# Weight loads of the software DMA queue over 15 engines instead of 14

## The chip, the cores and the metric

The kernel runs on one core of one Trainium2 chip. The metric is the device time of one execution in microseconds (us). Before the change it is 749.29 us, the median of three runs (747.64 to 749.32). A profiled execution is a run of its own, and its time stands beside its span below.

## The reference

For each of 1024 samples there are 32 fields of 128 numbers. For each of the 496 pairs of fields (i, j) with i < j there is a 128 x 128 weight matrix. Field i is multiplied by the matrix of the pair, and the result is multiplied, number by number, with field j. Everything is float32.

```python
v_i = inputs[:, I_IDX, :]
v_j = inputs[:, J_IDX, :]
transformed = jnp.einsum('bpd,ped->bpe', v_i, W)
return transformed * v_j
```

The output has 1024 x 496 x 128 numbers, 260 MB; inputs and weights together are 49 MB.

## The kernel before, in words

**Tiles.** The host lays the fields out as `xt` (32 fields, each 128 x 1024: embedding on the partitions, samples along the row) and the weights as `wt`: 62 chunks of 8 pairs, each chunk 128 partitions x 8 x 128, that is 4 KB a partition and 512 KB in all. A pair q is worked on in two halves of 512 samples; the loop variable u counts the halves, 992 of them. The output of four pairs is gathered in one tile `ot` (128 x 4 x 1024, 16 KB a partition) and stored with one transfer of 2 MB.

**Work on a pair.** From the 16th pair on, each matrix and each field is split into two parts whose products are exact enough: ScalarE and GpSimd make the parts of a weight chunk in `split_w` (L141 to L145), two pairs at a time, and those of a field in `split_x` (L159 to L161). `first` (L223) has TensorE do two matmuls into PSUM and ScalarE scale the sum; `second` (L239), three halves later, adds the third matmul, and VectorE multiplies the finished 128 x 1024 with field j into the output tile (L255). Stores are issued on ScalarE's queue two halves later (L282). The order of all of this is written out by hand in one loop (L264 to L298); nothing is reordered afterwards.

**Output tiles.** There are three fixed tiles and, for a part of the time, four more, which lie in the room of field groups that are loaded late (`XAT`, L38: at pairs 52, 141, 219 and 313 one of them begins to be filled with fields). So from seven at the start the number of output tiles falls to three. `out_tile` takes the one whose last use is longest ago; VectorE's write into it waits until its last store has landed.

**Weight loads.** Three buffers hold weight chunks. The first chunks are loaded at times fixed in `w_at`; from chunk 12 on a chunk is loaded when GpSimd has finished splitting the one whose buffer it takes (`ring`, `spent`, L288 to L296). A whole chunk is one transfer on SyncE's queue (L125): 128 rows of 4 KB. The 25 chunks in `WAPART` (12, 14, ... 60) are loaded in two parts by `load_apart` (L106): the first `ROWS` = 8 x 14 = 112 partitions by GpSimd's software queue (L107), with the source seen as 14 x 8 rows, and the last 16 partitions by SyncE (L108). The host reorders the rows of these chunks to match.

**The cursor.** `move_on(k)` (L102, L104) issues a small transfer on the software queue: 2k rows of 64 bytes into the tile `mark`, seen as k x 2 rows. Nothing reads `mark`. It is issued once with k = 5 before the first such load, with k = 16 - 14 = 2 a few pairs after every load but the last (the list `back`, filled in the ring's code with the pair number plus `BACK`), and with k = 13 after the last. The sum of all k and of all 14s is 416 = 26 x 16.

Of the kernel before, what the change touches and what calls it, by code (L numbers as in the profile page):

```python
# [30 lines left out]
XLEAD = 5  # L31

XG = 4
NE = 14
ROWS = 8 * NE
WAPART = tuple(range(12, 62, 2))
BACK = 3
# [13 lines left out]
def kernel(  # L51
# [22 lines left out]
    nc = tc.nc  # L74
# [12 lines left out]
    def load_x(f, pieces=1, eng=None):  # L87
        if f == 0:

            t = rpool.tile([P, WL, P], F32, tag="w", name="x_0").rearrange("p q e -> p (q e)")  # L90
        else:
            t = xpool.tile([P, BT], F32, tag=f"x{f}", name=f"x_{f}")
        s = BT // pieces
        for k in range(pieces):
            (eng or nc.sync).dma_start(out=t[:, k * s : (k + 1) * s], in_=xt[f, :, k * s : (k + 1) * s])
        x_sb[f] = t

    w_raw = {}

    mark = xpool.tile([32, 16], F32, tag="mark", name="mark")  # L100

    def move_on(k):  # L102

        nc.gpsimd.dma_start(out=mark[: 2 * k], in_=xt[0, : 2 * k, :16].rearrange("(b a) n -> a b n", a=k))  # L104

    def load_apart(dst, src):  # L106
        nc.gpsimd.dma_start(out=dst[:ROWS], in_=src[:ROWS].rearrange("(b a) m n -> a b m n", a=NE))  # L107
        nc.sync.dma_start(out=dst[ROWS:], in_=src[ROWS:])  # L108
# [3 lines left out]
    def load_group(k, m):  # L112
        if m == XG - 1:
            group[k] = xpool.tile([P, XG, BT], F32, tag=f"g{k}", name=f"x_g{k}")
        f = XG * k + 1 + m
        x_sb[f] = group[k][:, m, :]
        nc.sync.dma_start(out=x_sb[f], in_=xt[f])

    def load_w(c, splits=(0, WL), eng=nc.sync):
        w_raw[c] = rpool.tile([P, WL, P], F32, tag="w", name=f"w_{c}")  # L120
        if c in WAPART:
            load_apart(w_raw[c], wt[c])
            return
        for a, b in zip(splits, splits[1:]):
            eng.dma_start(out=w_raw[c][:, a:b, :], in_=wt[c, :, a:b, :])  # L125
# [97 lines left out]
    def first(u):  # L223
        q, h = divmod(u, 2)
        i, c = pairs[q][0], q // WC
        r = slice(q % WC * P, (q % WC + 1) * P)
        s = slice(h * HB, (h + 1) * HB)
        if h == 0:
            po[q] = ppool.tile([P, BT], F32, tag="po", name=f"po_{q}")
        if q < nq0:  # L230
            nc.tensor.matmul(po[q][:, s], w_raw[q // WL][:, q % WL, :], x_sb[i][:, s], start=True, stop=True)  # L231
        else:
            for t in (0, 1):
                m = nc.tensor.matmul(po[q][:, s], w_s[c][t][:, r], x_s[i][t][:, s], start=t == 0, stop=t == 1)  # L234
                apart(m, scaled.get(u - 1) if h else None)
            scaled[u] = nc.scalar.mul(po[q][:, s], po[q][:, s], 1.0 + EPS)  # L236
            apart(scaled[u], taken.get(q - PB), "TensorE's products, which this waits for, have waited for it")

    def second(u):  # L239
        q, h = divmod(u, 2)  # L240
        i, j = pairs[q]
        r = slice(q % WC * P, (q % WC + 1) * P)
        s = slice(h * HB, (h + 1) * HB)
        if q >= nq0:
            m = nc.tensor.matmul(  # L245
                po[q][:, s], w_s[q // WC][2][:, r], x_s[i][2][:, s], start=False, stop=True, skip_group_check=True
            )
            apart(m, scaled[u ^ 1])
        g, k = divmod(q, OG)
        if k == 0 and h == 0:  # L250
            ots[g] = out_tile(g)
        if q >= NQ - 2:
            nc.vector.tensor_tensor(ots[g][:, k, s], po[q][:, s], x_sb[j][:, s], ALU.mult)  # L253
        elif h == 1:
            taken[q] = nc.vector.tensor_tensor(ots[g][:, k, :], po.pop(q), x_sb[j], ALU.mult)  # L255
        if q >= NQ - 2:
            stores.append((u + SLAG, out[g, :, k, s], ots[g][:, k, s]))
        elif g == 0 or q >= NQ - OG:
            if h == 1:
                stores.append((u + SLAG, out[g, :, k], ots[g][:, k]))  # L260
        elif k == OG - 1 and h == 1:
            stores.append((u + SLAG, out[g], ots[g]))

    for u in range(2 * NQ + LAG + SLAG):  # L264
        q = u // 2
        if u < 2 * NQ:
            i, j = pairs[q]
            if u % 2 == 0 and j == i + 1 and XG * ngroup < i - 2 - XLEAD:
                load_x(i - 2 - XLEAD)
            first(u)  # L270
            if u == 2 * nq0:
                move_on(5)
            if u % 2 == 0 and q in group_at:
                load_group(*group_at[q])
            if u % 2 == 1 and q in w_at:
                load_w(w_at[q])
            if u % 2 == 0 and q in back:
                move_on(16 - NE if max(w_raw) < WAPART[-1] else 13)
        if LAG <= u < 2 * NQ + LAG:
            second(u - LAG)  # L280
        while stores and stores[0][0] <= u - LAG:
            nc.scalar.dma_start(*stores.pop(0)[1:])  # L282
        if u % 2 == 1:
            ready = [t for t in todo if t[0] <= q]
            if ready:
                ready[0][2](u)
                todo.remove(ready[0])
        if ring[WB:] and ring[0] in spent:  # L288
            ring.pop(0)
            c = ring[WB - 1]  # L290
            if c == "x":
                load_x(0)
            else:
                load_w(c)
            if c in WAPART:
                back.append(q + BACK)  # L296
        while later and later[0][0] <= u:
            nc.vector.tensor_tensor(*later.pop(0)[1:], ALU.subtract)  # L298
# [31 lines left out]
```

## Time and profile before

| | |
|---|---|
| median of three runs | 749.29 us |
| the profiled execution, its own time | 743.81 us |
| span of the profiled execution, first to last instruction | 742.0 us |
| mean granted TensorE clock | 0.991 |
| moved by DMA | 310.04 MB, 418 GB/s over the span |
| stores of 2 MB on ScalarE's queue | 122, 13.2 us from issue to landing (median) |
| weight loads on the software queue | 25 of 448 KB, 11.8 us to landing; issue 0.622 us of GpSimd |
| their rest on SyncE's queue | 25 of 64 KB, 6.1 us to landing |
| cursor moves on the software queue | 26, 9.8 us to landing; issue 0.637 us of GpSimd on average |

How to read the profile: it starts with the busy time of each engine, then shows the span in 40 slices. In the row DMA each digit is the mean busy share of the core's 16 DMA engines in tenths. Part 3 lists the DMA queues: q10 is ScalarE's, which carries the stores, q1 SyncE's, which carries most loads, q0 the software queue of GpSimd, q8 and q14 fetch instructions. A line of the waits reads: who waited, for whom, the time in total, how often, and the longest single wait in us. A line of the windows reads: the stretch, its length, each engine's busy time with its count of instructions (PE, PEld, DVE, ACT, POOL), the granted clock, the DMA share and GB/s. PE is TensorE, DVE VectorE, ACT ScalarE, POOL GpSimd, SP SyncE. The trace also has a record for every DMA packet (start, duration, queue, size; not the DMA engine that moved it) and the time of each of the 16 landings of every transfer.

### The profile page before, as it was taken

Reading aid. Unit: us, or ns where it says so; the run is one execution under the profiler, and the core shown is the slowest. Engines: PE = TensorE matmul, PEld = TensorE weight load, DVE = VectorE, ACT = ScalarE, POOL = GpSimd, SP = SyncE. Lnnn points to the kernel's source line nnn. Section 1 sums busy time; section 2 is a strip of 40 time slices with the busy share of each in tenths; the row PEclk is TensorE's granted clock in tenths of the full one; section 3 lists DMA queues with packets and bytes.
Section 4 is the critical chain, followed back from the end, with each engine's and each line's share of the span. In section 5 each row is a group of like instructions: output and inputs, shape, how many; then the busy total and the mean of one; then the engine's idle time right before and its main releaser. Section 6 shows DMA issues by size and latency. Waiting matters only on the chain.

```text
span 742.0 us, 10650 instructions
## 1 busy us (share of the span) xinstructions
PE 703.8 (95%) x2946; PEld 549.4 (74%) x2946; DVE 636.8 (86%) x550; ACT 634.9 (86%) x1256; POOL 594.8 (80%) x882
## 2 busy tenths in 40 slices
PE   7999999999999999999899979999999999999994
PEld 3577777777878887776687758867878778777783
DVE  4888999999999998987798868977999899888885
ACT  1298999999999999898899968988989999998893
POOL 1789999999999999887778866977797878797660
PEclk9999999999999999999999999999999999999998
DMA  9999999999999999999999998999999999999998
GB/s 347 427 424 428 427 427 425 430 423 426 427 419 426 423 424 425 425 423 422 425 428 422 428 423 334 420 423 423 423 425 422 426 423 415 430 421 422 424 408 351
DMA packets 34667, 310.04 MB, mean 418 GB/s; under 512 B 5296, under 2 KB 5424, under 8 KB 18992
## 3 DMA queue, kind: packets, MB, share of 16 engines
q10 hardware_dynamic: 19584, 261.10, 83.4%
q1 hardware_dynamic: 10592, 36.77, 12.3%
q0 software_dynamic: 4432, 11.48, 3.9%
q8 instruction: 24, 0.39, 0.2%
q14 instruction: 35, 0.29, 0.1%
HBM read 49.29 MB, written 260.05 MB: 417 GB/s over the span
## 4 chain that ended last, share of the span: by engine, by line
PE 61%; DMA 23%; DVE 8%; POOL 3%; issue 2%; ACT 1%; DVEq 0%; ACTq 0%; POOLq 0%
PE po L234 38%; DMA out_dram<-ot 23%; PE po L245 19%; DVE ot L255 6%; PE po L231 4%; DVE xd L298 2%; POOL wd L145 1%; POOL wl L143 1%; POOL xl L160 1%; ACT po L236 0%; DMA x<-in_xt_dram 0%; POOL xl L161 0%; POOL wd L144 0%; DVE ot L253 0%; ACT wh L141 0%
## 5 line engine op out<-in xcount | busy, mean ns | idle before, releaser
L236 ACT ACTIVATE po<-po 128x512 f32<-128x512 f32 x962 | 553.4, 584 | 76.3 <-PE po L234 60.3
L255 DVE TENSOR_TENSOR ot<-po,x 128x1024 f32<-128x1024 f32 x358 | 429.8, 1220 | 70.9 <-DMA out_dram<-ot 23.8
L234 PE MATMUL po<-xh,wh 128*128 128x512 f32 x962 | 382.4, 398 | 20.1 <-DVE ot L255 19.1
L245 PE MATMUL po<-xd,wd 128*128 128x512 f32 x962 | 376.3, 391 | 4.8 <-DVE ot L253 2.4
L234 PE MATMUL po<-xl,wl 128*128 128x512 f32 x962 | 377.1, 392 | 1.4 <-POOL wl L143 1.0
L234 PEld LDWEIGHTS po<-xh,wh 128*128 128x128 f32 x962 | 181.2, 188 | 78.3 <-DVE ot L255 41.7
L143 POOL TENSOR_TENSOR wl<-w,wh 128x256 fp32r<-128x256 f32 x241 | 185.2, 768 | 66.1 <-ACT wh L141 60.0
L245 PEld LDWEIGHTS po<-xd,wd 128*128 128x128 f32 x962 | 181.1, 188 | 45.2 <-DVE ot L253 3.2
L234 PEld LDWEIGHTS po<-xl,wl 128*128 128x128 f32 x962 | 181.3, 188 | 41.0 <-POOL wl L143 4.0
L145 POOL TENSOR_TENSOR wd<-wl,wd 128x256 fp32r<-128x256 f32 x241 | 181.4, 753 | 20.1
L255 DVE TENSOR_TENSOR ot<-po,x_g 128x1024 f32<-128x1024 f32 x136 | 164.0, 1222 | 25.9 <-DMA out_dram<-ot 9.7
L144 POOL TENSOR_SCALAR wd<-wh 128x256 fp32r<-128x256 f32 x241 | 101.9, 423 | 20.5
L141 ACT ACTIVATE wh<-w 128x256 fp32r<-128x256 f32 x241 | 98.7, 410 | 5.7 <-DVE ot L255 3.6
L298 DVE TENSOR_TENSOR xd<-xh,xl 128x512 fp32r<-128x512 f32 x52 | 48.5, 934 | 0.0
L160 POOL TENSOR_TENSOR xl<-x_g,xh 128x512 fp32r<-128x512 f32 x32 | 41.5, 1297 | 3.2 <-ACT xh L159 2.9
L160 POOL TENSOR_TENSOR xl<-x,xh 128x512 fp32r<-128x512 f32 x20 | 25.8, 1290 | 15.7 <-ACT xh L159 15.4
L161 POOL TENSOR_SCALAR xl<-xl 128x512 fp32r<-128x512 f32 x52 | 34.4, 662 | 4.6
L231 PE MATMUL po<-x,w 128*128 128x512 f32 x60 | 28.4, 630 | 3.9 <-DMA x<-in_xt_dram 3.9
L231 PEld LDWEIGHTS po<-x,w 128*128 128x128 f32 x60 | 11.6, 199 | 19.9 <-issue 13.7
L159 ACT ACTIVATE xh<-x 128x512 fp32r<-128x512 f32 x20 | 12.3, 624 | 11.4 <-DMA x<-in_xt_dram 11.3
L159 ACT ACTIVATE xh<-x_g 128x512 fp32r<-128x512 f32 x32 | 20.0, 624 | 0.0
L104 POOL DMA_DIRECT2D mark<-in_xt_dram x26 | 16.6, 637 | 0.0
(7 smaller groups left out, 19.9 us busy)
## 6 DMA issues: line engine op xcount, KB each, us to landing
out_dram<-ot ACTq DMA_DIRECT2D x122, 2048.0 KB, 13.2
w<-in_wt_dram SPq DMA_DIRECT2D x36, 512.0 KB, 11.1
w<-in_wt_dram POOLq DMA_DIRECT2D x25, 448.0 KB, 11.8
x_g<-in_xt_dram SPq DMA_DIRECT2D x16, 512.0 KB, 17.0
x<-in_xt_dram SPq DMA_DIRECT2D x14, 512.0 KB, 9.5
out_dram<-ot ACTq DMA_DIRECT2D x6, 512.0 KB, 8.3
w<-in_wt_dram SPq DMA_DIRECT2D x26, 64.0 KB, 6.1
x<-in_xt_dram ACTq DMA_DIRECT2D x4, 256.0 KB, 5.7
```

The costliest lines, as they stand in the source:

```text
L141: halved[c] = nc.scalar.mul(h, raw, 1.0 - 2.0**-13)
L143: nc.gpsimd.tensor_tensor(l, raw, h.bitcast(F32), ALU.subtract)
L144: nc.gpsimd.tensor_scalar(d, h.bitcast(F32), EPS, 1.0, ALU.mult, ALU.mult)
L145: nc.gpsimd.tensor_tensor(d, l.bitcast(F32), d.bitcast(F32), ALU.subtract)
L160: nc.gpsimd.tensor_tensor(l, x_sb[f][:, s], h.bitcast(F32), ALU.subtract)
L161: nc.gpsimd.tensor_scalar(l, l.bitcast(F32), 1.0 / EPS, 1.0, ALU.mult, ALU.mult)
L231: nc.tensor.matmul(po[q][:, s], w_raw[q // WL][:, q % WL, :], x_sb[i][:, s], start=True, stop=True)
L234: m = nc.tensor.matmul(po[q][:, s], w_s[c][t][:, r], x_s[i][t][:, s], start=t == 0, stop=t == 1)
L236: scaled[u] = nc.scalar.mul(po[q][:, s], po[q][:, s], 1.0 + EPS)
L245: m = nc.tensor.matmul(po[q][:, s], w_s[q // WC][2][:, r], x_s[i][2][:, s], start=False, stop=True, skip_group_check=True)
L255: taken[q] = nc.vector.tensor_tensor(ots[g][:, k, :], po.pop(q), x_sb[j], ALU.mult)
L298: nc.vector.tensor_tensor(*later.pop(0)[1:], ALU.subtract)
```

## The change

The number of engines `NE` goes from 14 to 15. With it `ROWS` becomes 120, so GpSimd's queue loads 120 partitions of a split chunk, seen as 15 x 8 rows, and SyncE's queue the last 8. The move after each load becomes `move_on(1)`, for which a branch of its own issues a transfer of one number (4 bytes); the last move becomes 12 instead of 13. The first stays at 5. The host's reordering follows `NE`.

```diff
-NE = 14
+NE = 15
 ROWS = 8 * NE
...
     def move_on(k):
 
-        nc.gpsimd.dma_start(out=mark[: 2 * k], in_=xt[0, : 2 * k, :16].rearrange("(b a) n -> a b n", a=k))
+        if k == 1:
+            nc.gpsimd.dma_start(out=mark[:1, :1], in_=xt[0, :1, :1])
+        else:
+            nc.gpsimd.dma_start(out=mark[: 2 * k], in_=xt[0, : 2 * k, :16].rearrange("(b a) n -> a b n", a=k))
...
             if u % 2 == 0 and q in back:
-                move_on(16 - NE if max(w_raw) < WAPART[-1] else 13)
+                move_on(16 - NE if max(w_raw) < WAPART[-1] else 12)
```

## The prediction

> **What bounds the kernel now.** I read the page's slices first, then the DMA part, the waits, the critical chain, and last the packet records and landings of the trace.
>
> ```profile
> span 742.0 us, 10650 instructions
> PE 703.8 (95%) x2946; PEld 549.4 (74%) x2946; DVE 636.8 (86%) x550; ACT 634.9 (86%) x1256; POOL 594.8 (80%) x882
> ...
> DMA  9999999999999999999999998999999999999998
> ...
> q10 hardware_dynamic: 19584, 261.10, 83.4%
> q1 hardware_dynamic: 10592, 36.77, 12.3%
> q0 software_dynamic: 4432, 11.48, 3.9%
> ```
>
> The DMA row is 9 in all slices but two, and the three data queues fill 99.6% of the 16 engines. PE is at 95%, but the waits say that it is held, through DVE, by stores that have not yet landed:
>
> ```profile
> PEld po L234 <- DVE ot L255: 41.7, 58, 5.8
> DVE ot L255 <- DMA out_dram<-ot: 33.5, 32, 6.3
> PE po L234 <- DVE ot L255: 19.1, 24, 5.4
> ```
>
> A store lands only when its last engine is done, so the slowest engine matters, not the mean. The DMA view of 125 to 440 us gives the rate and the depth of the queue:
>
> ```profile
> DMA packets 13999, 133.73 MB, mean 425 GB/s; under 512 B 2340, under 2 KB 2340, under 8 KB 6992
> ...
> out_dram<-ot ACTq DMA_DIRECT2D x55, 2048.0 KB, 17.3
> ```
>
> A store of 2 MB is issued every 315 / 55 = 5.7 us and lands 17.3 us after its issue: three are in flight at a time, and no engine runs dry.
>
> The records name no engine, but a packet's start follows the end of the one before it on its engine by -4, -3 or 2 ns, and each engine must do 8 rows of every store. That lets me put the packets of 64 to 440 us into sixteen chains, none with an idle gap over 20 ns. What they show:
>
> - fourteen chains: a 16 KB store row takes 611 ns in the median, 613.6 in the mean; a 4 KB row 159 ns.
> - the two chains that get no rows of the split weight loads (I call them S and T; they also carry the two packets of the cursor move). S is slow before any load is split (64 to 125 us: mean 626 ns, against 612 on the others) and after (648). T is as fast as the others before (615, median 611); after, the mean is 649 with the median still 611: it is held now and then.
> - what S and T lost to long packets from 125 to 440 us is 16.9 and 16.7 us; of the others none lost over 2.9. The relief in that time is 14 loads x 7 rows x 0.155 us = 15.2 us. So T's relief goes into being held, and S's pays for its slowness: S stays 2 to 4 rows behind the median chain from 150 us on.
>
> At 435 us a straggler (one of the fourteen, 6 to 7 rows behind) holds a store, DVE waits 6.3 us, and PE comes back at a lower clock:
>
> ```profile
> 435.00:440.00 5.00, 2.56 (x12) 1.78 (x10) 0.42 (x1) 3.14 (x7) 4.50 (x9) 1.00 0.98 414
> 440.00:445.00 5.00, 2.02 (x5) 1.65 (x6) 3.28 (x4) 0.58 (x1) 0.43 (x1) 0.65 1.02 437
> 445.00:450.00 5.00, 5.00 (x17) 3.95 (x16) 2.90 (x3) 2.85 (x6) 0.79 (x2) 0.66 0.50 213
> ```
>
> The columns after the engines are clock, DMA share and GB/s. So late landings cost time here; the fourteen loaded engines and S set the pace together.
>
> **What the Trainium skill says.** All from the page DMA: Bandwidth & Descriptors.
> - Section "Why a DMA increments its semaphore by 16 and not by 1": the slowest dimensions of the two access patterns give the number k of engines; the software queue takes k consecutive ones from a round-robin cursor, SP's and ACT's queues the lowest-numbered k. The trace agrees for the software queue: fourteen chains with 8 rows per load, the same two without, and five chains with a marker at 36 us, both S and T among them. If the cursor starts at 0, the first move of 5 marks engines 0 to 4, the loads skip 3 and 4, and {S, T} = {3, 4}; no run shows the start.
> - Section "Queues, rings and completion order": an engine takes its queues in turn, by packets. The trace agrees: in a chain the rows of q0 and q1 stand between those of q10. A row more on one engine is then time more on it.
> - Section "Latency and other measured facts": engines 7 and 15 are usually the slower ones, with a guessed cause. The trace has one such chain, S, and no number for it.
> - Section "Where 436 GB/s comes from": a ceiling of 435 GB/s; 425 here, 98% of it.
>
> **The change, part by part.**
> 1. Instructions. The order on every engine is the same; shapes alone differ. POOL's issues of the load and of the move keep their places: 25 x 0.622 us and 26 x 0.637 us. The 4-byte move may cost less than the 4 rows or as much; nothing says more, 24 x (-0.1 to +0.1) us = -2.4 to +2.4 us on POOL, which is busy 80%. I take 0; what covers it is POOL's lead on its weight splits: PE waited for them for 4.0 + 1.0 us in all. Uncovered it would cost those 2.4 us at most. SP issues 8 rows instead of 16 (0.326 us each, on an otherwise idle queue): nothing. The move waits for the marker before it, 22 us old with a landing of 9.8: no wait, and the weight splits queued behind it on POOL are not held.
> 2. Rows. Per load of 128 rows, before: fourteen engines 8 + 1, two engines 1. After: fifteen engines 8, one none, and SP's 8 rows on engines 0 to 7, one each. So engines 0 to 7 keep 9 (the spared one 1), engines 8 to 15 go from 9 to 8, and the engine that loses its relief goes from 1 to 9: + 25 x 8 x 0.155 = 31 us of packets. The upper eight lose 25 x 0.155 = 3.9 us each. The sum of bytes is the same.
> 3. Who loses the relief. After the first move of 5, a load of 15 skips only the fifth of the marked engines, and 15 + 1 = 16 brings the cursor back to the same place, so it is always that one; the fourth now gets rows. The fourth is S or T.
> 4. If it is S. A loaded chain's nominal work: 122 stores x 8 x 0.607 = 592.5; 66 whole loads x 8 x 0.155 = 81.8; 25 x 9 x 0.155 = 34.9; small ones 14: 723 us. S's own slowness, from 64 to 125 us where it has no relief: 15 ns on 976 store rows = 14.6, 7 ns on about 800 rows of 4 KB = 5.6, 20 us in all. With some 3 us of instruction fetches on it (queues 8 and 14: 24 x 0.95 + 32 x 0.31 us over sixteen engines is 2.0) S needs 746 us of packets. The fourteen need 723 + 2 of fetches + 4 of long packets (1.5 us in 315, over 742) = 729 now and the span is 742, so 13 us are start, the stall at 440 us and the tail. If S can use those 13 us, the span is 749; if it meets as much idle time, 759; if the rate of 648 ns (37 ns x 976 = 36 us) also holds without relief, 775. I take 757: after 313 pairs only three output tiles are left, so S's lag stops the others and is not made up. That is +15 us on 742.0; the profiled execution took 743.8, so 759. The median shown is 749.3, 5.5 above that execution; I carry the difference over: 764.
> 5. If it is T. It gets 31 us of rows in place of 33 us of being held (16.7 us in 315, over the 617 us left), and is again a fast chain: 0. The upper eight's 3.9 us count only if the straggler is among them.
>
> The stall that step 4 removes from the others (they now wait for S) moves, it doesn't go: next behind S stands PE, 98 of 100 us busy from 100 to 300 us.
>
> **The rivals.**
> - *The relief stays with S* (T loses it). For: no gap in any chain, and T fast before the split. Against: nothing but the unknown number. Ends at 749, 747 to 751.5: not slower. It decides by one thing, whether S is the fifth of the marked engines or the fourth, and that is even.
> - *The same, and the straggler lies in the upper half.* It gains up to 3.9 us, about the 3.6 to 5.0 us by which the last of a store's 16 landings trails the middle ones from 340 to 435 us, and the stall of 6.3 us with its slow clock goes: 743 to 747. For: 8 of 16 places. Against: such stalls come from instruction fetches too, which stay.
> - *The cursor doesn't move by one.* Then the unloaded engine wanders, each is relieved once or twice in 25 loads, and S loses nearly all its relief: as in step 4, 764. For it: 4 bytes on one engine are not in this trace. Against: the moves by 2 and 5 mark exactly 2 and 5 chains.
> - *T is slow too once loaded beside S's relief*, with a quarter to a third of the 36 ns by which its mean lies over the others': x 976 rows = 9 to 12 us, less the 3 us that the engines stood still at 446 us: 755 to 758. For it: that mean. Against: its 615 ns before the split.
>
> **How the numbers follow.** S loses the relief (wandering cursor included): 0.50, 764 (757 to 772). Relief stays with S and nothing else: 0.19. Stays, with the straggler helped: 0.20. T slow too: 0.11. The profile makes S-or-T even; the first case is the likeliest single one because the other half divides. Measurements of this kernel can tell about 0.3% (2.2 us) from no change. Faster 0.20, same 0.18, slower 0.62. From 744 to 772 us about 2 in 10 are left out: the far ends of steps 4 and of the straggler's case. The slower cases' own range is 755 to 772.
>
> **What would show it.** Right: one chain without weight rows instead of two, a chain of about 626 ns or more per store row among those with rows, the last landing of stores more than 5 us behind the median, DVE waiting for stores well over 33.5 us, GB/s below 420 from 125 to 700 us. Wrong: the slow chain is the one without rows, and the waits are as before. A mistake in step 4's rate (626 or 648 ns) moves the size by 16 us, not the sign.

## The result, and the profile after

| | before | after |
|---|---|---|
| median (lowest to highest) | 749.31 us, 4 runs (747.64 to 749.44) | 757.33 us, 4 runs (756.88 to 757.72) |
| profiled execution, its own time | 743.81 us | 757.06 us |
| its span, mean clock | 742.0 us, 0.991 | 755.2 us, 0.985 |

The ratio is 1.0126 with an interval of 1.0102 to 1.015; the medians lie 8.0 us apart, the change being slower. The two profiled executions lie 13.2 us apart, since that of before was 5.5 us below its median and that of after is at its own.

The head of the page, its DMA slices and its queues:

```profile
span 755.2 us, 10650 instructions
...
PE 710.3 (94%) x2946; PEld 550.8 (73%) x2946; DVE 634.4 (84%) x550; ACT 636.2 (84%) x1256; POOL 597.7 (79%) x882
...
DMA  9999999999999999999999997999999999999998
...
q10 hardware_dynamic: 19584, 261.10, 82.3%
q1 hardware_dynamic: 10192, 35.95, 12.1%
q0 software_dynamic: 4432, 12.30, 4.4%
```

The work is the same: as many instructions, and each engine's busy time within 7 us. q1 has 400 packets less, which is 25 loads x (8 rows + 8 landings): SyncE's part runs on eight engines instead of sixteen. The time is in the waits (who, for whom: us in total, times, longest):

```profile
PEld po L237 <- DVE ot L258: 50.0, 64, 6.1
DVE ot L258 <- DMA out_dram<-ot: 44.6, 39, 6.6
PE po L237 <- DVE ot L258: 24.6, 32, 5.7
```

DVE waits 11.1 us more for stores (33.5 before), and PE for DVE 8.3 + 5.5 us more in its two queues. The same three waits as before, each longer; no new one. The windows of after show the two longest waits (columns: stretch, length, PE, PEld, DVE, ACT, POOL with counts, clock, DMA share, GB/s):

```profile
295.00:300.00 5.00, 3.47 (x16) 2.54 (x14) 1.23 (x1) 4.30 (x9) 4.58 (x8) 1.00 1.00 420
300.00:305.00 5.00, 1.19 (x3) 1.00 (x4) 2.35 (x2) 0.00 (x0) 1.84 (x4) 0.71 1.02 433
305.00:310.00 5.00, 5.00 (x16) 3.92 (x15) 3.11 (x4) 2.78 (x6) 0.05 (x1) 0.60 0.88 377
...
445.00:450.00 5.00, 1.17 (x6) 0.63 (x4) 0.00 (x0) 1.79 (x4) 3.44 (x6) 0.89 1.02 434
450.00:455.00 5.00, 3.13 (x7) 2.51 (x8) 4.18 (x4) 1.11 (x2) 0.00 (x0) 0.50 0.32 134
455.00:460.00 5.00, 5.00 (x22) 4.10 (x21) 3.68 (x3) 3.91 (x9) 2.32 (x4) 0.93 0.45 190
```

Before had one such place, at 440 us. Now there are two, at 300 and at 447 us. At each, PE, DVE and ACT run dry while the DMA engines work at full rate (433 and 434 GB/s), and then the clock is 0.5 for 6.8 us (from 302.1 and from 448.9 us). At the second the stores that weren't computed in time are missing afterwards, and the DMA engines run dry too (134 GB/s). The timelines of VectorE name what it waited for (in brackets: the idle time before, and what ended it), first of after at both places, then of before:

```profile
302.53 2.35 DVE L258 TENSOR_TENSOR ot<-po,x 128x1024 f32<-128x1024 f32 x2 [6.19 <-DMA out_dram<-ot]
...
450.59 2.36 DVE L258 TENSOR_TENSOR ot<-po,x 128x1024 f32<-128x1024 f32 x2 [6.56 <-DMA out_dram<-ot]
```

```profile
295.96 2.36 DVE L255 TENSOR_TENSOR ot<-po,x 128x1024 f32<-128x1024 f32 x2 [2.56 <-DMA out_dram<-ot]
...
441.71 2.36 DVE L255 TENSOR_TENSOR ot<-po,x 128x1024 f32<-128x1024 f32 x2 [6.29 <-DMA out_dram<-ot]
```

Counting VectorE's multiplications shows that these are pair 196 and pair 292, in both kernels. By the program, pair 196 begins the first output tile that is chosen from four instead of five, and pair 292 the first that is chosen from three instead of four. The tile taken there was stored one store later than usual, so late landings that had cost nothing until then are waited for at once. The wait at pair 292 is nearly the same before and after. The one at pair 196 has grown from 2.6 to 6.2 us.

The issue times of the stores tell how much each place cost. With the stores of 2 MB counted from 0, number 10 (at 86 us) is issued 2.2 us later than before; this is earlier than the first split load (128 us), and in the profiled executions number 10 comes at 84.3 to 86.4 us, whatever the kernel. Number 47 (296 us) is 2.9 us late, number 48 (310 us, the tile of pair 196) 8.9, number 72 (457 us, the tile of pair 292) 8.2, number 104 10.6 and number 121 12.2. So some 9 of 13 us are lost by 310 us, 6 of them at pair 196; pair 292 adds nothing to the difference, and the other four come after it. There VectorE's waits for stores are many and short: from 460 us on 26 of at most 1.6 us, 20.9 us in all, where before has 18 with 14.9. (e9 below starts as early as the kernel before and is still 8.5, 7.8 and 11.7 us late at numbers 48, 72 and 121, so the late start isn't what sets the end.)

The landings show why that tile is late. Every store has sixteen landings; the table gives, as means over the stores issued in a stretch, how far the last lies behind the median landing and, after the stroke, behind the last but one (us):

| issued | before | after |
|---|---|---|
| 125 to 200 us | 2.4 / 0.7 | 2.3 / 1.0 |
| 200 to 260 | 2.5 / 0.4 | 5.2 / 3.2 |
| 300 to 350 | 4.0 / 1.5 | 7.3 / 5.6 |
| 400 to 440 | 4.2 / 2.7 | 10.0 / 7.7 |

After the change one engine alone is late up to 440 us, and by the second number no other is near it. (From 500 to 700 us, behind the dry stretch at 450, the last landing is only 0.6 to 1.4 us behind the last but one.) The packet chains say which. In 63 to 310 us the chain that is slow before any load is split (632.8 ns a store row, 636.0 later; the other fifteen 614.5) falls behind the median chain by 2 rows at 134 us, 5 at 198, 6.5 at 246 and 11 at 294 us. Eleven rows of 0.611 us are 6.7 us, about the wait of 6.2 us at pair 196. That is S. In the kernel before it stayed within 4 rows. S now gets weight rows like the others.

They also say what the prediction didn't hold likeliest: the chain without rows is not always the same. In the first split load it is S; in the second it is another, and so on. SyncE's 8 rows are on eight chains alone, which the prediction took to be engines 0 to 7; this tells lower from upper chains: the chain without rows is a lower one in the first five loads and an upper one in the next three. This fits engines 4, 3, 2, 1, 0, 15, 14, 13: down by one with each load, just what follows when the loads take 15 consecutive engines and the transfer of 4 bytes doesn't move the cursor. S is then relieved in loads 1 and 17 only (at 128 and 506 us), in 2 of 25.

### The profile page after: what moved, and what is told of

The parts are those of the page before. It is cut to its first block, busy times and chain, and to the rows that moved or that the text cites. A ratio compares the mean times of both kernels' runs of the same rounds, so it can differ in the third digit from the quotient of the medians.

```text
span 755.2 us, 10650 instructions
## 1 busy us (share of the span) xinstructions
PE 710.3 (94%) x2946; PEld 550.8 (73%) x2946; DVE 634.4 (84%) x550; ACT 636.2 (84%) x1256; POOL 597.7 (79%) x882
## 4 chain that ended last, share of the span: by engine, by line
PE 51%; DMA 30%; DVE 8%; POOL 5%; issue 2%; ACT 2%; ACTq 0%; DVEq 0%; POOLq 0%
PE po L237 32%; DMA out_dram<-ot 30%; PE po L248 15%; DVE ot L258 7%; PE po L234 4%; DVE xd L301 1%; POOL wl L146 1%; POOL wd L148 1%; POOL xl L163 1%; ACT po L239 1%; DMA x<-in_xt_dram 1%; POOL wd L147 1%; POOL xl L164 1%; ACT wh L144 0%; DVE ot L256 0%
## 5 line engine op out<-in xcount | busy, mean ns | idle before, releaser
L147 POOL TENSOR_SCALAR wd<-wh 128x256 fp32r<-128x256 f32 x241 | 103.7, 430 | 20.5
L301 DVE TENSOR_TENSOR xd<-xh,xl 128x512 fp32r<-128x512 f32 x52 | 46.0, 885 | 0.0
L234 PE MATMUL po<-x,w 128*128 128x512 f32 x60 | 30.3, 664 | 4.1 <-DMA x<-in_xt_dram 4.0
L234 PEld LDWEIGHTS po<-x,w 128*128 128x128 f32 x60 | 12.3, 212 | 21.2 <-issue 15.1
L162 ACT ACTIVATE xh<-x 128x512 fp32r<-128x512 f32 x20 | 12.3, 624 | 11.5 <-DMA x<-in_xt_dram 11.4
L110 POOL DMA_DIRECT2D w<-in_wt_dram x25 | 17.0, 680 | 0.0
```

The lines of the kernel that those rows point to most:

```text
L147: nc.gpsimd.tensor_scalar(d, h.bitcast(F32), EPS, 1.0, ALU.mult, ALU.mult)
```

## The experiments

The theory after the result: the transfer of 4 bytes leaves the cursor where it is, the row-less engine wanders, and S, with rows in 23 loads, holds the stores. The rivals: the cursor does move, and the relief simply went to the wrong engine of the two or T counts as well; or 15 engines cost something for themselves (rows, GpSimd's longer issues).

**A real move by one, first attempt: e1_two_moves and e2_spare_fourth.** Moves by 9 and by 8 come to 17, which is one. The second kernel also starts with 4 instead of 5 (and ends with 13), so that the spared engine is the fourth of the marked ones. Edit to the kernel after:

```diff
-                move_on(16 - NE if max(w_raw) < WAPART[-1] else 12)
+                for k in (9, 8) if max(w_raw) < WAPART[-1] else (12,):
+                    move_on(k)
```

> The change with its move of 1 (4 bytes) replaced by a move of 9 and one of 8, 17 in all, so that the cursor surely goes on by 1; the last move stays 12. Theory A (the 4-byte transfer leaves the cursor where it is, so the engine without rows wanders and the slow engine S loses its relief): the engine without rows is the same one at all loads, the fifth of the marked ones, which is S; the time goes back to that of before, 747 to 750 us, although T has rows now. Theory B (the loss comes from 15 engines instead of 14, T's lost relief, or SyncE's 8 rows on only eight engines): the time stays at 756 to 758 us. The second move costs GpSimd 24 x 0.6 = 15 us of its own time, which is covered in both theories.

> As the run with two moves, but the first move is 4 instead of 5 and the last 13 instead of 12: the engine without rows is the one below, T, at all loads, and S has rows in all 25. Theory A: slower than before and somewhat slower than the change, whose wandering relief still reaches S in 2 of 25 loads: 757 to 764 us. Theory B (which of the engines is relieved doesn't matter): the same as the run with two moves.

Measured: 894.79 us (ratio 1.1918, 1.1839 to 1.1997) and 896.9 us (1.196, 1.1895 to 1.2025), far from anything expected. The waits of e1_two_moves:

```profile
POOL mark L107 <- DMA mark<-in_xt_dram: 153.9, 21, 12.7
PEld po L237 <- POOL wl L146: 145.9, 25, 11.2
PE po L237 <- POOL wl L146: 135.6, 25, 10.8
```

Both moves write the tile `mark`, so the second waits on GpSimd until the first has landed, 7.3 us on average; the weight splits stand behind it in GpSimd's order, and PE waits for them. The pair of moves was not the harmless edit that it was taken for, and both runs say nothing on the question. They show what the prediction's step 1 had looked at: a move after a move into the same tile is free only if the older one has landed.

**No relief at all: e3_whole_loads.** The kernel before with `WAPART = ()` and without moves: all weights in whole chunks on SyncE's queue, 8 rows of each on every engine.

```diff
-WAPART = tuple(range(12, 62, 2))
+WAPART = ()
...
-            if u == 2 * nq0:
-                move_on(5)
...
-                move_on(16 - NE if max(w_raw) < WAPART[-1] else 13)
+                pass
```

> The kernel before with no split loads: WAPART is empty, all weight chunks go over SyncE's queue on all 16 engines, and there is no cursor move. Theory A: S has no relief at all and all others one row less per load (3.9 us in all): 755 to 761 us, like the change. Theory B (the change loses by something of its own): 748 to 752 us, or much like before.

Measured: 753.75 us (753.52 to 754.23, 20 runs), ratio 1.0075 (1.0057 to 1.0093). Whole loads are slower than the kernel before and faster than the change. The last landing trails the last but one by 6.2 us (200 to 260 us) and 7.2 us (400 to 440 us), where before has 0.4 and 2.7: without relief there is a single late engine. Splitting is worth 5 us against this, and the change makes a split that is worth less than none.

**A move of 17 rows: e4_move_17_rows.** If it is the 4 bytes that leave the cursor alone, more rows should move it. The run took it that 17 rows, which can't be shared out evenly, go to one engine.

```diff
-            nc.gpsimd.dma_start(out=mark[:1, :1], in_=xt[0, :1, :1])
+            nc.gpsimd.dma_start(out=mark[:17], in_=xt[0, :17, :16])
```

> The change with the 4-byte transfer replaced by one of 17 rows of 64 bytes. [...] If a transfer on one engine never moves the cursor: the engine without rows wanders down by one per load as in the change, 756 to 758 us. If only the single number leaves the cursor alone: the engine without rows is fixed at S and the time is 747 to 750 us. If 17 rows are spread over more engines, the cursor moves by another number, and the time is 752 to 760 us.

Measured: 757.69 us (757.46 to 758.01), ratio 1.0103 (1.005 to 1.0156), the same as the change; the row-less chain is another one in each load here too, S first, then four more of the lower ones, then upper ones. So the 4 bytes are not the only transfer that leaves the cursor where it is. But the rows did not go to one engine: in each of the eight moves from 130 to 290 us the packets show two rows (128 bytes) on each of eight chains and the last row (a packet of 68 bytes) on a ninth, always the same nine, the eight with SyncE's rows among them. The run therefore says nothing on transfers that use one engine. Nor does the change: there every chain has a packet of 4 bytes in each move, and the trace doesn't tell on which of them the number went.

**A real move by one, second attempt: e5_two_marks and e6_two_marks_fourth.** As the first attempt, but the move by 8 has a tile of its own. e6 again begins with 4 and ends with 13: there the fourth of the marked engines, T, is spared, and S has rows in every load.

```diff
-    mark = xpool.tile([32, 16], F32, tag="mark", name="mark")
+    marks = [xpool.tile([32, 16], F32, tag=f"mark{n}", name=f"mark{n}") for n in (0, 1)]
...
+                    move_on(9)
+                    move_on(8, marks[1])
```

> The run with moves of 9 and 8 again, but the second move writes a tile of its own, so it no longer waits on GpSimd for the first one to land (that wait cost 154 us). 15 engines have rows, the same one, the fifth marked engine, has none. Theory A (the change loses because its 4-byte transfer leaves the cursor alone and S loses its relief): the time of before within 0.3%, or up to 4 us below it. Theory B (15 engines, T's lost relief or SyncE's 8 rows on eight engines cost it): 0.8 to 1.3% slower than before, as the change.

> As the run with two marks, with a first move of 4 and a last of 13: the engine without rows is T, the neighbour below, and S has rows in all 25 split loads. Theory A: slower than the run with two marks by 1 to 1.5%, at or above the change, 757 to 764 us. Theory B: the same time as the run with two marks, whatever that is.

Measured, against 748.03 us for the kernel before: e5 748.26 us (742.98 to 753.04, 22 runs), ratio 0.9981 (0.9958 to 1.0005); e6 760.31 us (759.99 to 760.69), ratio 1.017 (1.0134 to 1.0207). VectorE's wait for stores, in e5 and in e6:

```profile
DVE ot L258 <- DMA out_dram<-ot: 29.6, 27, 5.9
```

```profile
DVE ot L258 <- DMA out_dram<-ot: 45.3, 42, 6.6
```

Both kernels use fifteen engines and move by one; the only difference is which engine goes without rows. With S spared the stores are waited for less than before the change (33.5), with S loaded as much as in the change (44.6). These are sums of one execution each and rank the kernels only roughly: e8 below, as fast as the kernel before, has 39.5. What shows the cause is the times. In e6 the row-less chain is the same in successive loads. In e6 the last landing of the stores at 400 to 440 us trails the last but one by 8.8 us, in e5 by 2.6.

**Which of the two spared engines counts with 14: e7_spare_5_6 and e8_spare_4_5.** The kernel before with another first move (and the last one to match): 7 spares the sixth and seventh engine, neither S nor T; 6 spares S and the one above it, and T gets rows.

```diff
-                move_on(5)
+                move_on(7)
```

```diff
-                move_on(5)
+                move_on(6)
```

> The kernel before (14 engines, moves of 2) with a first move of 7 and a last of 11: the two engines without rows are the two above S, neither S nor T. Theory A: slower than before by 1 to 1.5%, 756 to 764 us, since S has rows in every load, though 14 engines are used and nothing else of the change is in it. Theory B (the number of engines matters): the time of before.

> The kernel before with a first move of 6 and a last of 12: the engines without rows are S and the one above it instead of S and T. Theory A: the time of before within 0.3%, since only S's relief counts. If T needs its relief too: 750 to 756 us.

Measured against 748.03: e7 759.92 us (759.4 to 760.17), ratio 1.0163 (1.0126 to 1.0199); e8 747.26 us (744.08 to 754.84, 22 runs), ratio 1.0007 (0.9985 to 1.0028). The wait in e7:

```profile
DVE ot L255 <- DMA out_dram<-ot: 52.5, 48, 6.6
```

So S without relief costs 12 us with 14 engines as with 15 (11.9 and 12.3), and T's relief is worth nothing that these runs can tell in either (e5, e8). S is the fifth of the engines that the first move marks, T the fourth.

**The change without its moves: e9_no_move.** The 24 transfers of 4 bytes are left out; nothing reads what they write.

```diff
-                move_on(16 - NE if max(w_raw) < WAPART[-1] else 12)
+                if max(w_raw) >= WAPART[-1]:
+                    move_on(12)
```

> The change without its 24 transfers of 4 bytes; the first move of 5 and the last of 12 stay. If those transfers leave the cursor where it is, they do nothing: the time of the change, 757 to 758 us, 1.2 to 1.3% over before, and the engine without rows goes down by one with each load. If they did move the cursor by some other number, the wandering is another one and the time can differ: 754 to 760 us.

Measured: 756.8 us (756.53 to 757.13), ratio 1.0117 (1.0066 to 1.0168). The change has 757.33 and 1.0126. With and without its moves the kernel takes the same time: they neither help nor cost. PE's waits for weight splits, 4.3 + 0.9 us in the change (4.0 + 1.0 before), are gone in e9, and this shows nowhere in the time: while S sets the pace, GpSimd's issues are covered.

**How much relief S can use: e10_thirteen_loads, e11_seven_loads and e12_thirteen_of_before.** e5 with fewer split loads, every second (13) and every fourth (7) of them; e12 is the kernel before with the first of these two edits, one line.

```diff
-WAPART = tuple(range(12, 62, 2))
+WAPART = tuple(range(12, 62, 4))
```

> The run with two marks, where only every second of the 25 chunks is loaded in two parts (chunks 12, 16, ... 60: 13 loads), the others whole over 16 engines. S gets 13 + 12 x 8 = 109 rows in place of 25, the others 8 rows more seldom 9. If S is ahead of need with its full relief (the time against rows of S was 748 at 25, 754 at 200, 760 at 225, which is steeper at the end): 745 to 748 us, the same as before or up to 2 us below. If time rises in proportion to S's rows from 25 on: 752 to 753 us.

> As the run with 13 loads, with only every fourth of the 25 split (12, 20, ... 60: 7 loads): S gets 7 + 18 x 8 = 151 rows. If S only binds above about 170 rows: 746 to 749 us. If time rises in proportion: 754 to 755 us.

> The kernel before, 14 engines and moves of 2, with only every second of its 25 chunks loaded in two parts (13 loads; the last move stays 13). S and T get 13 + 12 x 8 = 109 rows each, the other fourteen 9 x 13 + 8 x 12 = 213 instead of 225. If the gain of the run with 13 loads on 15 engines (0.74%) comes from fewer rows on the engines that bind once S is cared for: 742 to 745 us here too, at most a little above that run, whose upper eight engines have 200 rows. If it needs T to take its share: 746 to 749 us, as before.

Measured: e10 742.17 us (741.54 to 747.4, 13 runs) against 748.94, ratio 0.9926 (0.9902 to 0.995); e11 747.4 us, ratio 0.9985 (0.9963 to 1.0007); e12 745.2 us (741.94 to 750.72, 22 runs) against 748.71, ratio 0.9956 (0.9935 to 0.9978). e10 and e12 beat both kernels. Whether 15 engines with a real move are better than 14 isn't told by them: the intervals of e10 and e12 overlap. The profiled execution of e10 has a span of 739.7 us, 2.3 less than that of before, and VectorE waits less for stores:

```profile
DVE ot L258 <- DMA out_dram<-ot: 28.6, 29, 6.4
```

But fewer split loads are also fewer issues on GpSimd, which holds the weight splits. PE's waits for them, in e5 and in e10:

```profile
PEld po L237 <- POOL wl L146: 8.3, 14, 2.0
...
PE po L237 <- POOL wl L146: 3.1, 4, 1.6
```

```profile
PEld po L237 <- POOL wl L146: 1.9, 3, 1.1
...
PE po L237 <- POOL wl L146: 0.7, 1, 0.7
```

The kernel before has 4.0 and 1.0, e12 0.3 and none. From store number 10 to number 40, a stretch in which VectorE never waits for a store, e5 takes 174.1 us and e10 170.5, the kernel before 170.2 and e12 168.9. So 3.6 of the 6.1 us between e5 and e10, and 1.4 of the 3.5 between before and e12, are there before any store is waited for. These are single executions, and no run parts the two causes.

All kernels by the 4 KB rows that S carries in the 25 loads (9 in a split load with rows on S, 1 in one without, 8 in a whole one):

| S's rows | kernels | median us |
|---|---|---|
| 25 x 1 = 25 | before; e5; e8 | 748.0 to 749.3; 748.3; 747.3 |
| 13 x 1 + 12 x 8 = 109 | e10; e12 | 742.2; 745.2 |
| 7 x 1 + 18 x 8 = 151 | e11 | 747.4 |
| 25 x 8 = 200 | e3 | 753.8 |
| 23 x 9 + 2 x 1 = 209 | the change; e4; e9 | 757.3; 757.7; 756.8 |
| 25 x 9 = 225 | e6; e7 | 760.3; 759.9 |

From 109 rows on the time grows with the rows: by 18.1 us for 116 rows from e10 to e6, by 14.7 us from e12 to e7, which is 0.16 and 0.13 us a row, about the duration of one packet of 4 KB (0.159). It doesn't grow evenly (3.6 us for the 9 rows from e3 to the change, 6.4 for the 49 from e11 to e3), since the kernels differ in their split loads as well. With fewer rows than 109 it grows again. GpSimd's issues are one likely cause of this, by the waits above. That the other DMA engines then set the pace, since they carry for S, is another, and not shown; what a split adds for them is small (in the kernel before 9 rows in place of 8 on each of fourteen engines).

## Why the prediction was right, and where it was wrong

Forecast 764 us, measured 757.33: slower by 8.0 us, where 14.7 were forecast. The main case, "S loses the relief (wandering cursor included)", is what happened, and the way from there to the time, a loaded S that holds the stores, was the one named. But S lost the relief in another way than steps 3 and 4 have it. There the cursor moves by one and S is the fourth marked engine; in the runs the cursor stands still and S is the fifth. With S the fifth and a cursor that moves by one, S would have kept its relief. In so far the case held by luck: the wandering had been counted into it although the prediction argued against it. And 757.33 lies at the lower end of the main case's 757 to 772 and within the 755 to 758 of "T is slow too" as well; e5 to e8 tell the two apart, not the number. The steps:

- **Step 1, instructions at nothing: right.** The 4-byte move takes 612 ns on GpSimd, the moves of before 637 on average; the load's issue 0.680 us in place of 0.622, 1.4 us over 25 loads. PE's waits for weight splits are 4.3 + 0.9 us, 4.0 + 1.0 before, and e9, without the moves, is as fast. "The move waits for the marker before it, 22 us old": shown, as the view of the tile `mark` has no idle time before any of them. In the first line below the columns are durations (least, median, greatest) and the first and last start:

```profile
L105 POOL DMA_DIRECT2D mark<-in_xt_dram x24: 607/612/617, 130.4 to 673.5; - x24
...
its engine sat idle before it (us, times) until:
who waited for it (us, times):
```

- **Step 2, rows: right per load.** The engine that loses its relief gets 8 rows more, but in 23 loads, not 25: 28.5 us of packets, not 31.
- **Step 3, "15 + 1 = 16 brings the cursor back to the same place, so it is always that one": failed.** The rival "The cursor doesn't move by one" holds, shown by the chains and by e9. The section "Why a DMA increments its semaphore by 16 and not by 1" of the Trainium skill's page DMA: Bandwidth & Descriptors says that the software queue takes k consecutive engines from a round-robin cursor and that a transfer of one number gets one engine. The runs agree for moves by 2 and 4 to 7, for 9 and 8 together and for loads by 14 and 15, each of which put the relief where this rule has it. After the transfer of one number the cursor stood still, and the measurement decides; that the number went to one engine is not seen in the trace. The argument against the rival, "the moves by 2 and 5 mark exactly 2 and 5 chains", was about other values of k: it could not speak for the one untried. Had step 3 held, the kernel would have been about e5: 748.26 us, no change, the first rival's 749. (e5 has twice the moves, and PE waits 8.3 + 3.1 us for weight splits in it, so the kernel meant here could be somewhat faster.)
- **Step 4, the size: the span right, the sum on top wrong.** "If it is S": it is T that is the fourth, but the sum holds for any way by which S is loaded. "I take 757" is the span for an S with rows in every load: e6 has 758.8 and e7 757.6. Its parts were less good: S's store rows took 21.5 ns more than the others' (636.0 against 614.5), not 15, so its slowness is 21.5 x 976 + 5.6 us = 26.6 us and not 20. The rest of the span, for idle time on S, is then some 6 us in e6, not the 11 that the step took: two errors that cancel. What missed is "the median shown is 749.3, 5.5 above that execution; I carry the difference over". That difference belongs to the kernel before, whose runs range over 743 to 755 us. Where S alone sets the pace the times repeat within 1 us (e3: 20 runs in 753.52 to 754.23), and the profiled execution is a typical one (e6: 760.66 against a median of 760.31). Without that term the step gives 759, with the 2 loads that relieve S (2 x 8 x 0.155 = 2.5 us) 756.5; measured 757.33.
- "**After 313 pairs only three output tiles are left, so S's lag stops the others**": by the program three are left from pair 292 on, and the lag costs most a step sooner, at pair 196, where five tiles become four and 11 rows of lag are waited for at once. After pair 292 four more us are lost in short waits.
- **Step 5, T at nothing: right** (e5 and e8).
- "**The stall ... moves, it doesn't go**": it didn't move. It stayed at pair 292 (6.3 us before, 6.6 after), and it is there in e5 with S relieved as well (6.0 us), so it isn't S's. The rival that had it vanish when the upper eight engines have a row less is not borne out by e5 either. What S's lag made is the long wait at pair 196.
- **What would show it:** S's store rows above 626 ns, the last landing over 5 us behind the median (from 200 to 440 us), DVE's wait well over 33.5 us came out. The rate came out in part: 420 GB/s over 125 to 440 us, 388 in 400 to 500, 410 in 600 to 700. "One chain without weight rows instead of two" is so in each load, but not over the loads.

**What stays open.** The number of the engine S follows from the order of the row-less chains only if SyncE's 8 rows are on engines 0 to 7, as the prediction took it: it's then 4, and the cursor stood at 0 when the kernel started. No record names an engine. Why the cursor stays after 4 bytes and after 17 rows, why S is slower, why T is held while it runs ahead, and why kernels with S relieved differ from run to run by some 10 us, was not found.

## What to carry to other kernels

When every transfer is spread over all the engines, the slowest one sets the pace: read the last landing against the last but one, and if a single engine trails, move its rows, and try how many: here half the relief was 3.5 to 6.8 us faster than all of it, and some of that seems to come from fewer issues on GpSimd. A lag costs nothing until a buffer must be free; look for it where the number of buffers falls. A change of spread must say which engine gains and which loses; the sum of bytes and the mean rate don't show it. Before relying on a scheduling rule at a value that the trace doesn't hold (here k = 1), look for the way to get the same effect with values that it does hold (9 + 8 = 17).

## What the runs showed of the hardware that was not expected

- A transfer of 4 bytes on the software queue didn't advance the queue's cursor, and one of 17 rows, which lay on nine engines, didn't either (the change 757.33 us, e4 757.69, without moves 756.8). Transfers seen as k x 2 rows with k of 2 and 4 to 7, or of 9 and 8 together, and loads seen as 14 or 15 x 8 rows did, by k.
- One engine takes 636 ns for a 16 KB store row where the others take 614.5, 3.5% more, and its place, the fifth of the first move's engines, was the same in all kernels, on four chips. The prediction had from the Trainium skill (DMA: Bandwidth & Descriptors, "Latency and other measured facts") that engines 7 and 15 are usually the slower ones; this one is among the eight that carry SyncE's 8 rows and, if these are 0 to 7, is 4 and not 7.
- After VectorE's waits of 6.2 and 6.6 us in the change PE gets half its clock for 6.8 us. The Trainium skill's page TensorE: Matmul & The Clock Gate, section "Part 1: The HAM clock gate (the "warmup" mystery)", has half the clock after an idle window of about 3.4 us, and full clock after a busy one; the trace agrees, with twice that length, and in e6 and e10 also with a single one (3.4 us at 305.3 and at 299.6 us). A late store is so paid for twice; the wait of 2.6 us at pair 196 in the kernel before left the clock at 1.00.
- Two transfers into one tile on GpSimd's queue: in e1 the second waits on GpSimd until the first has landed, 154 us over 21 waits; with a tile each, in e5, there is no such wait.
